# A second mixture of experts in which half of the tokens go to one expert per 128-row tile

## The chip, the cores and the metric

The kernel runs on one core of one Trainium2 chip. The metric is the device time of one launch in microseconds. The engines are called as the profile calls them: PE (matrix products and transposes), PEld (loading of PE's stationary operand), DVE and ACT (elementwise work), POOL (GpSimd), SP (the engine whose queue issues most DMAs). Everything is float32.

## The reference

The reference is a decoder of two layers on x of shape (32, 128, 128): 4096 tokens of 128 features. Each layer is an attention, a cross attention to a context of the same shape, and a mixture of experts, each behind a layer norm and added to x. Only the second layer's mixture matters here:

```
def _L1_ffn_ref(...):                      # x: layer norm of the tokens, (4096, 128)
    scores = x @ gate_w.T                  # (4096, 16); the 4 best experts of each token,
    ...                                    # a softmax over their 4 scores
    routed = sum over the 4 of  share * silu(x @ w1[e].T) * (x @ w3[e].T) @ w2[e].T
    shared = silu(x @ sw1.T) * (x @ sw3.T) @ sw2.T
    return routed + shared                 # 16 experts, all matrices 128 x 128
```

## The kernel before

A token block is 128 tokens, a group (`GB`) four blocks, 512 tokens; there are 8 groups, `x[0]` to `x[7]`, which stay in SBUF by token (128 partitions of tokens). The program runs in four stages on all groups: the first layer's two attentions (`first_layers`), its mixture (`mixture_layer`), the second layer's attentions (`second_layers`), and its mixture (`mixture_layer` again, the last stage).

`steps` writes a stage's order: each entry is (function, first step, every how many steps, how many times), and `between` entries fill in one vector operation at a time. In `second_layers`, from step 8 on, the order of PE, DVE, ACT and POOL is kept as it is written (`manual_schedule`); elsewhere the framework orders instructions by readiness and by their place in the program. Every engine, and SP's queue, works in order: an instruction that waits holds all behind it.

The second mixture (`mixture("l1f", ...)`) has these parts:

- `norm`, `scaled`, `turn`: the layer norm of a group (`bn_stats` on DVE, `power` on POOL, scaling half on DVE and half on POOL at L1106), and its transposes to features by tokens, `hx`.
- `routing` and `choose`: the products with the gate for two groups at a time (`NBR` = 8 blocks), and some 40 small DVE operations (`route_softmax`, `pick`) that find the four best of 16 experts and their shares. A generator is advanced a few operations per step.
- `send` and `fetch`: the shares are transposed, written to DRAM (`combined`) and read back, broadcast over 128 partitions (`share`, 1 MB per DMA).
- `experts(u)`: half a group's experts. For each of the 16 experts, and the shared one, on all 512 tokens of the group: two products of 512 columns into `pg` and `pu`, Silu on ACT (L1849), times `pu` on DVE (L1850), times the shares on DVE (L1852), and a third product that accumulates in `y`. After the last, `x` is added to `y` by four products with the identity, ACT copies and stores.

So every expert computes every token and the shares of the 12 not chosen are zero. The routing of groups 0 and 1 is done inside `second_layers`; that of the other groups inside the last stage, one pair of groups ahead. W1F, the weights of this mixture (3.3 MB), is loaded to SBUF once, before `second_layers`.

Of the kernel before, what the change touches and what calls it, by code (L numbers as in the profile page):

```python
# [17 lines left out]
GB = 4  # L18
# [57 lines left out]
def _layout(i):  # L76
# [44 lines left out]
        "later": {"b_o": rows(i["L1_xattn_b_o"], D), **_by_position("cos1", "sin1")},  # L121
# [820 lines left out]
def fast_decoder(ctx: ExitStack, tc: tile.TileContext, ins, spans, out: bass.AP):  # L942
# [6 lines left out]
    st = ctx.enter_context(tc.tile_pool(name="st", bufs=4))  # L949
    kinds = {}  # L950
# [8 lines left out]
    def mm(*args, **kw):  # L959
        last[0] = nc.tensor.matmul(*args, **kw)  # L960
# [29 lines left out]
    F = load("fast", nc.sync)  # L990
    ident = K["ident"]


    def load_wide(eng, *names):
        t = res.tile([128, sum(ins[n].shape[1] for n in names)], F32, name="wide")
        at, out = 0, []
        for n in names:
            part = t[:, at : at + ins[n].shape[1]]
            at += ins[n].shape[1]
            out.append((_Pieces(part, spans[n]), lambda part=part, n=n: eng.dma_start(out=part, in_=ins[n])))  # L1000
        return out

    (W0X, load_w0x), (W0F, load_w0f) = load_wide(nc.sync, "w0x", "w0f")
# [18 lines left out]
    ones_by_4 = res.tile([128, 4, 4 * HD], F32, name="ones_by_4")  # L1022
# [67 lines left out]
    def moments(src):  # L1090

        n = src.shape[1]
        parts = st.tile([128, n, 6], F32, name=f"parts{n}")
        mv = st.tile([128, n, 2], F32, name=f"mv{n}")
        for b in range(n):
            nc.vector.bn_stats(parts[:, b, :], src[:, b, :])
            nc.vector.bn_aggr(mv[:, b, :], parts[:, b, :])
            yield
        return mv
# [22 lines left out]
    def norm_factors(g):  # L1122
        mv = yield from moments(x[g])
        return mv, power(mv[:, :, 1], 1e-5, -0.5, "r")
# [488 lines left out]
    def first_layers(after):  # L1613
# [7 lines left out]
        rnorm, rscaled, rturn, routing, choose, send, _, _ = after  # L1621
# [42 lines left out]
                (lambda _: choose(0, 5), 30, 1, 11),  # L1664
                (xnormalize, 12, 2, NW, xweights),
# [7 lines left out]
    def pick(v, n, k, desc):  # L1673

        m = v.shape[1]
        eq = st.tile([128, m, n], F32, name=f"eq{n}", bufs=2)
        top = st.tile([128, m], F32, name=f"top{n}", bufs=2)
        for _ in range(k):
            nc.vector.tensor_reduce(top, v, AX.X, ALU.max)
            yield  # L1680
            nc.vector.tensor_tensor(eq, v, rep(top, n, 2), ALU.is_equal)
            yield
            nc.vector.tensor_tensor(eq, eq, rep(desc, m, 1), ALU.mult)
            yield
            nc.vector.tensor_reduce(top, eq, AX.X, ALU.max)
            yield
            nc.vector.tensor_tensor(eq, eq, rep(top, n, 2), ALU.is_equal)
            yield
            nc.vector.scalar_tensor_tensor(v, eq, -BIG, v, ALU.mult, ALU.add)
            yield  # L1690
# [77 lines left out]
    def mixture(tag, W, route, per, last):  # L1768
# [5 lines left out]
        xn, hs, combs, choices, weights, shares = {}, {}, {}, {}, {}, {}  # L1774

        def norm(wk, g):
            xn[g] = yield from norm_factors(g)

        def scaled(wk, g):
            xn[g] = yield from normed(wk, g, *xn[g])  # L1780

        def turn(wk, g):
            pool = edge if g in groups(0) else wk
            hs[g] = pool.tile([128, GT], F32, name="hx", bufs=2 if g in groups(0) else 5)
            by_feature(xn.pop(g), hs[g])

        def routing(wk, n):
# [4 lines left out]
            choices[n] = route(lg, edge)  # L1792
# [40 lines left out]
        def experts(wk, u):  # L1833

            g, half = divmod(u, 2)
            if half == 0:
                ys[g] = sums([128, GT], "y")
            y, h = ys[g], hs[g]
            for c in range(nch // 2) if half == 0 else range(nch // 2, nch + 1):
# [13 lines left out]
                mm(y, lhsT=wd, rhs=sg, start=(c == 0), stop=(c == nch and not last))  # L1853
            if half == 0:
                return
# [14 lines left out]
        return norm, scaled, turn, routing, choose, send, fetch, experts  # L1870

    def mixture_layer(tag, stages, more=()):
# [3 lines left out]
            lambda k, stage=stage: stage(wk, k) for stage in stages  # L1876
# [215 lines left out]
    def second_layers(stages, early, late, after):  # L2092
# [5 lines left out]
        rnorm, rscaled, rturn, routing, choose, send, _, _ = after  # L2098
        R = NBR // GB
# [3 lines left out]
        of_four = lambda stage, b, at: (lambda g: stage(g * GB + b), at + b, 4, NG)  # L2103

# [20 lines left out]
            (first(routing), 25, 1, 1),  # L2125
            (first(send), 43, 1, 1, choose),
# [7 lines left out]
                (lambda _: choose(0, 3), 26, 1, 13),  # L2134
            ],
            as_written=8,
        )

# [34 lines left out]
    edge = ctx.enter_context(tc.tile_pool(name="edge", bufs=1, reuse_waits="tile"))  # L2173
    flag = res.tile([1, 1], I32, name="flag")
    mixture0 = mixture("l0f", W0F, route_groups, 2, False)
    with scope():
        first_layers(mixture0)
    with tc.tile_pool(name="l1early", bufs=1, reuse_waits="tile") as early:
# [13 lines left out]
        ((W1F, load_w1f),) = load_wide(nc.sync, "w1f")  # L2192
        load_w1f()
        mixture1 = mixture("l1f", W1F, route_softmax, 1, True)
        with scope():
            second_layers(stages, early, late, mixture1)
    with scope():
        mixture_layer("l1f", mixture1, ((lambda wk, _: not_ok(wk), 9, 1, 1),))
# [35 lines left out]
```

## Time and profile before

| | us |
|---|---|
| median of 3 runs (lowest, highest) | 1500.13 (1499.58, 1506.42) |
| the profiled execution | 1502.94 |
| its span, first to last instruction | 1501.1 |
| mean granted PE clock | 0.963 of full |

The span by stage, from the trace, in us:

| stage | from | to | PE busy | DVE busy | POOL busy |
|---|---|---|---|---|---|
| second attention layers (from the load of W1F on) | 830 | 1112 | 240 | 181 | 108 |
| second mixture | 1112 | 1494 | 379 | 213 | 14 |
| end | 1494 | 1501 | 1.6 | 0 | 0 |

In the profile's groups a line reads: line, engine, operation, out<-in by the program's names, partitions x elements, count | busy us, mean ns of one | idle time of that engine just before them, and what ended it. Nearly all products have line L960, since one helper issues them. In the table of stretches the columns are the window, its length, each engine's busy time with its count, PE's granted clock, the busy share of the 16 DMA engines and GB/s. In the timeline the columns are start, duration, engine, line, operation. SPq is SP's queue, which issues DMAs; its rows give min/median/max duration in ns of the issue.

### The profile page before, as it was taken

To read this page: it belongs to the slowest core of one execution; us is meant where nothing else is said; L and a number is where in the kernel's file an instruction comes from. 1 tells how busy PE (TensorE), PEld (TensorE's weight loads), DVE (VectorE), ACT (ScalarE), POOL (GpSimd) and SP (SyncE) were. 2 spreads that over 40 slices of the span, in tenths; PEclk is the share of its full clock that TensorE was granted. 3 is DMA by queue.
4 is the path that set the end of the run, shared out by engine and by line. 5 is a ranking of instruction groups with operands and counts; after the bars stand their busy time and mean duration, and the time that the engine had idled before them with its cause. 6 is when DMAs were issued, how large, how long until landed. Compare 5 with 4: busy or idle time off the path is not lost.

```text
span 1501.1 us, 25599 instructions
## 1 busy us (share of the span) xinstructions
PE 1381.5 (92%) x10288; PEld 818.0 (54%) x10288; DVE 927.8 (62%) x2299; ACT 574.6 (38%) x842; POOL 355.3 (24%) x549
## 2 busy tenths in 40 slices
PE   3699999999999996999999898898689999999998
PEld 1367777777777775444444555565344444444443
DVE  5656767768686643757745466777556564564454
ACT  2354545454454332232322355555342222222221
POOL 5324343333422311320001254533330100000000
PEclk7799999999999997899999999999799999999999
DMA  6001211111121124351350100000022221322210
GB/s 242 1 1 30 57 31 30 30 30 31 30 49 39 30 49 105 71 114 41 74 114 13 78 2 2 2 2 2 2 115 98 96 96 70 121 84 93 107 75 9
DMA packets 36766, 85.01 MB, mean 57 GB/s; under 512 B 3232, under 2 KB 20128, under 8 KB 32160
## 3 DMA queue, kind: packets, MB, share of 16 engines
q1 hardware_dynamic: 35200, 80.68, 18.7%
q10 hardware_dynamic: 1440, 2.61, 0.5%
q8 instruction: 83, 1.36, 0.4%
q14 instruction: 43, 0.35, 0.1%
HBM read 80.40 MB, written 2.88 MB: 55 GB/s over the span
## 4 chain that ended last, share of the span: by engine, by line
PE 72%; DVE 14%; POOL 4%; ACT 4%; DMA 3%; issue 2%; SPq 1%; DVEq 0%; ACTq 0%; POOLq 0%
PE y L960 13%; PE pu L960 11%; PE pg L960 11%; PE po L960 7%; PE pqk L960 5%; PE scores L960 4%; PE sums L960 3%; PE xscores L960 3%; PE pval L960 2%; DMA factor<-factors 2%; PE proj L960 2%; PE xsums L960 1%; ACT e L1260 1%; DVE v L1525 1%; POOL xn L1106 1%
## 5 line engine op out<-in xcount | busy, mean ns | idle before, releaser
L1850 DVE TENSOR_TENSOR sg<-sg,pu 128x512 f32<-128x512 f32 x208 | 142.8, 687 | 223.1 <-PE pu L960 219.3
L1849 ACT ACTIVATE sg<-pg 128x512 f32<-128x512 f32 x208 | 124.2, 597 | 375.5 <-PE pg L960 356.6
L960 PE MATMUL y<-sg,wide 128*128 128x512 f32 x416 | 222.1, 621 | 4.2 <-DVE sg L1852 2.4
L960 PE MATMUL pg<-hx,wide 128*128 128x512 f32 x416 | 215.8, 601 | 0.0
L960 PE MATMUL pu<-hx,wide 128*128 128x512 f32 x416 | 214.8, 598 | 0.0
L1260 ACT ACTIVATE e<-scores 128x1024 f32<-128x1024 f32 x128 | 124.0, 1021 | 55.4 <-PE scores L960 55.4
L960 PEld LDWEIGHTS y<-sg,wide 128*128 128x128 f32 x416 | 64.7, 188 | 131.4 <-DVE sg L1852 107.4
L1852 DVE TENSOR_TENSOR sg<-sg,share 128x512 f32<-128x512 f32 x192 | 132.5, 690 | 4.8
L960 PEld LDWEIGHTS pu<-hx,wide 128*128 128x128 f32 x416 | 79.1, 192 | 95.2 <-issue 93.6
L960 PEld LDWEIGHTS pg<-hx,wide 128*128 128x128 f32 x416 | 78.1, 192 | 89.7 <-issue 87.9
L1106 POOL TENSOR_SCALAR xn<-x,mv,r 128x128 f32<-128x128 f32 x96 | 80.6, 847 | 158.0 <-PE pxn L1115 82.8
L1275 DVE STREAM_TRANSPOSE by_token<-sums 128x512 f32<-128x512 f32 x64 | 45.6, 713 | 81.3 <-PE sums L960 81.0
L1511 ACT ACTIVATE e<-xscores 128x1024 f32<-128x1024 f32 x64 | 62.0, 1021 | 79.9 <-PE xscores L960 79.9
L960 PE MATMUL scores<-qb,k 32*128 32x512 f32 x512 | 75.5, 660 | 11.4 <-ACT qb L1446 4.0
L960 PE MATMUL sums<-e,v 128*32 128x128 f32 x2048 | 73.8, 285 | 12.7 <-POOL v L1056 10.6
L960 PEld LDWEIGHTS sums<-e,v 128*32 128x32 f32 x2048 | 54.7, 113 | 40.5 <-issue 15.0
L1525 DVE COPY v<-pval 128x512 f32<-128x512 f32 x64 | 43.5, 680 | 50.6 <-PE pval L960 50.6
L960 PE MATMUL po<-e,v 128*64 128x128 f32 x1024 | 65.0, 279 | 7.6 <-DVE v L1525 7.6
L1559 ACT COPY av<-po 128x512 f32<-128x512 f32 x64 | 37.5, 586 | 88.3 <-PE po L960 88.3
L960 PE MATMUL po<-av,wide 128*128 128x256 f32 x256 | 64.1, 406 | 7.7 <-DVE av L1579 7.7
L1490 DVE COPY qk<-pqk 128x512 f32<-128x512 f32 x64 | 43.4, 685 | 39.8 <-PE pqk L960 39.6
L1115 PE MATMUL pxn<-in_few,xn 128*128 128x128 f32 x192 | 37.0, 302 | 33.3 <-DVE xn L1106 21.9
(218 smaller groups left out, 2237.2 us busy)
## 6 DMA issues: line engine op xcount, KB each, us to landing
share<-combined SPq DMA_DIRECT2D x32, 1024.0 KB, 4.7
factor<-factors SPq DMA_DIRECT2D x64, 256.0 KB, 4.9
share<-combined SPq DMA_DIRECT2D x32, 512.0 KB, 12.0
wide<-in_w1f_dram SPq DMA_DIRECT2D x1, 3272.0 KB, 10.4
wide<-in_w0x_dram SPq DMA_DIRECT2D x1, 2112.0 KB, 10.4
x<-in_xt_dram SPq DMA_DIRECT2D x8, 256.0 KB, 5.5
ctx<-in_ctx_dram SPq DMA_DIRECT2D x8, 256.0 KB, 8.1
out_dram<-y ACTq DMA_DIRECT2D x8, 256.0 KB, 2.0
```

Source lines behind the costliest of these rows:

```text
L960: last[0] = nc.tensor.matmul(*args, **kw)
L1106: eng.tensor_scalar(n[:, b, :], x[g][:, b, :], mv[:, b, 0:1], r[:, b : b + 1], ALU.subtract, ALU.mult)
L1115: nc.tensor.transpose(pt[:, b, :], n[:, b, :], ident)
L1260: nc.scalar.activation(e[-1], ps[:, bass.ts(n, 2)].rearrange("p c i s -> p (c i) s"), AF.Exp, scale=scale)
L1275: nc.vector.transpose(tt.rearrange("p i t r -> p (i t r)"), po.rearrange("p i s -> p (i s)"))
L1490: nc.vector.tensor_copy(t, ps)
L1511: nc.scalar.activation(e[-1], ps[:, n].rearrange("p r c s -> p (r c) s"), AF.Exp, scale=scale)
L1525: nc.vector.tensor_copy(v[:, bass.ts(n, XC), :], pv)
L1559: nc.scalar.copy(avs[w][n][:, :, bass.ts(b, S)], po)
L1849: nc.scalar.activation(sg, pg, AF.Silu)
L1850: nc.vector.tensor_tensor(sg, sg, pu, ALU.mult)
L1852: nc.vector.tensor_tensor(sg, sg, shares[g][c // NS][:, c % NS], ALU.mult)
```

## The change

Groups 0 to 3 (`BY_ROWS` = 4 groups, 16 blocks) no longer go through all experts. Each of their tokens is written four times, by indirect DMA, to rows of a DRAM buffer ordered by expert, each expert's rows starting at a multiple of 128. That makes at most 4 x 16 + 16 = 80 tiles of 128 rows (`NT`), each of one expert, in 20 `QUADS` of four; the number is fixed whatever the routing. A quad is loaded, its four experts' matrices are loaded from DRAM by an expert number that SP reads into a register, and the results go to a second DRAM buffer. From there each token's four rows are gathered by indirect DMA, weighted with the shares and added to `x`. The shared expert and the store of these groups follow. Groups 4 to 7 go through all experts as before.

```diff
+    def filled(q):                                     # 20 of these, in first_layers, one a step from step 14
+        nc.sync.dma_start(out=four_tiles(rows_in, q), in_=rep(ident, 4, 1))
...
+        def route(lg, n):                              # for blocks 0 and 1 (groups 0 to 3)
...
+            for k in range(4):
+                yield from pick(v, E, 1, K["desc16"], ones[:, k, at])
+                t = st.tile([128, NBR, E], F32, name=f"eq{E}", bufs=2)
+                nc.vector.tensor_tensor(t, ones[:, k, at], s, ALU.mult)
+                nc.vector.tensor_reduce(raw[:, :, k], t, AX.X, ALU.add)
...
+        def places(_):                                 # row of each token and choice, expert of each tile
+            pos = sm([128, NB + 1, E], "places")
+            mm(pos, lhsT=L["below"], rhs=mask, start=True, stop=False)
+            for b in range(NB):
+                mm(pos[:, b + 1 :], lhsT=one.to_broadcast([128, 128]), rhs=rep(mask[:, b], NB - b, 1), ...)
...                                                     # some 20 DVE operations on 128x256
+        def way_out(u):                                # u: block, 0 to 15, after the steps of second_layers
...
+            nc.vector.tensor_scalar(t, x[g][:, b, :], mv[:, b, 0:1], r[:, b : b + 1], ALU.subtract, ALU.mult)
+            for k in range(4):
+                sent = nc.gpsimd.indirect_dma_start(
+                    out=rows_in,
+                    out_offset=bass.IndirectOffsetOnAxis(ap=place[:, k, u : u + 1], axis=0),
+                    in_=t, in_offset=None)
...
+        def weights(wk, q):                            # all on SP's queue, kept in this order
+            xq = wk.tile([128, 4, D], F32, name="rows", bufs=3)
...
+                sent = nc.sync.dma_start(out=xq, in_=four_tiles(rows_in, q))
+            for j in range(4):
+                with tc.issue_after(sent.ins):
+                    e = nc.sync.value_load(owner[0:1, 4 * q + j : 4 * q + j + 1], min_val=0, max_val=E - 1)
+                    w = wk.tile([128, 3, S], F32, name="row_weights", bufs=12)
+                    sent = nc.sync.dma_start(out=w, in_=every[:, :, bass.ds(e, 1), :].rearrange("p k e f -> p (k e) f"))
...
+        def experts(wk, q):
+            for j in range(4):
+                nc.tensor.transpose(pt[:, j], xq[:, j], ident)
+            nc.vector.tensor_copy(h, pt)
+            for i, p in enumerate((pg, pu)):
+                for j, w in enumerate(ws):
+                    mm(p[:, j], lhsT=w[:, i], rhs=h[:, j], start=True, stop=True)
+            nc.scalar.activation(sg, pg, AF.Silu)
+            nc.vector.tensor_tensor(sg, sg, pu, ALU.mult)
+            for j, w in enumerate(ws):
+                mm(py[:, j], lhsT=sg[:, j], rhs=w[:, 2], start=True, stop=True)
+            nc.scalar.copy(y, py)
+            nc.scalar.dma_start(out=four_tiles(rows_out, q), in_=y)
...
+        def way_back(wk, u):
+            t = wk.tile([128, 4, D], F32, name="back", bufs=4)
+            for k in range(4):
+                nc.gpsimd.indirect_dma_start(out=t[:, k], out_offset=None, in_=rows_out,
+                    in_offset=bass.IndirectOffsetOnAxis(ap=place[:, k, u : u + 1], axis=0))
+            for k in range(4):
+                nc.vector.scalar_tensor_tensor(xb, t[:, k], share[:, u, k : k + 1], xb, ALU.mult, ALU.add)
...
+    def last_layer(tag, stages, rows_stages):          # in place of mixture_layer for the second mixture
+        steps(                                         # G0 = 4, R = 2, n = 3
+            (lambda i: fetch(G0 + i), 0, 1, 1),
+            (lambda i: turned(G0 + R + i), 0, 1, R),   # norm, scaled, turn of groups 6, 7
+            (lambda _: fetch(G0 + 1), 0, 1, 1),
+            (lambda _: routing(n), 1, 1, 1),
+            (lambda _: stages[4](n), 1, 1, 1),
+            (again, 1, 1, G0),                         # scaled and turn of groups 0 to 3 once more
+            (lambda _: send(n), 3, 1, 1),
+            (lambda i: fetch(G0 + R + i), 3, 1, R),
+            (weights, 4, 1, QUADS),
+            (row_experts, 4, 1, QUADS),
+            (way_back, 4 + QUADS, 1, NB),
+            (lambda u: experts(2 * G0 + u), (0, 1, 2, 3, 4 + QUADS, 8 + QUADS, 12 + QUADS, 16 + QUADS), 1, 2 * (NG - G0)),
+            (shared, 8 + QUADS, 4, G0),
+            (rest, 8 + QUADS, 4, G0),
+            (lambda _: not_ok(wk), 6, 1, 1),
+        )
...
     def second_layers(stages, early, late, after, rows_stages):
-        R = NBR // GB
+        R = BY_ROWS + NBR // GB                        # norm, scaled, turn of 6 groups here, not 2
...
-            (first(routing), 25, 1, 1),
-            (first(send), 43, 1, 1, choose),
+            (first(routing), 25, 8, 3),
+            (places, 38, 1, 1, choose_1),
+            (lambda _: send(early, 2), 44, 1, 1, choose_2),
...
-                (lambda _: choose(0, 3), 26, 1, 13),
+                (lambda _: choose(0, 8), 26, 1, 6),
+                (choose_1, 34, 1, 4),
+                (choose_2, 42, 1, 3),
             ],
             as_written=8,
         )
+        for u in range(NB):
+            way_out(u)
```

Not shown: three small constant tables are added to a load, some buffers move between pools, and the layer norm's factors of groups 0 to 3 are kept for `way_out` and `again`.

## The prediction

> **What bounds the kernel now.** I read the page first, then busy time by stage, then the last stage's groups, then single rows for the prices of what the change adds.
>
> ```profile
> span 1501.1 us, 25599 instructions
> PE 1381.5 (92%) x10288; PEld 818.0 (54%) x10288; DVE 927.8 (62%) x2299; ACT 574.6 (38%) x842; POOL 355.3 (24%) x549
> ...
> PE 72%; DVE 14%; POOL 4%; ACT 4%; DMA 3%; issue 2%; SPq 1%; DVEq 0%; ACTq 0%; POOLq 0%
> ```
>
> PE carries 72% of the chain that ended last; POOL is idle for three quarters of the span.
>
> ```profile
> core 0: us, PE busy (x) PEld busy (x) DVE busy (x) ACT busy (x) POOL busy (x), PEclk, DMA share, GB/s
> 830.00:1112.00 282.00, 240.34 (x3094) 157.78 (x3094) 180.76 (x522) 146.14 (x198) 108.18 (x171) 0.95 0.02 5
> 1112.00:1494.00 382.00, 378.89 (x970) 161.34 (x971) 212.70 (x397) 101.67 (x165) 14.02 (x19) 1.00 0.25 94
> 1494.00:1501.00 7.00, 1.62 (x10) 1.05 (x8) 0.00 (x0) 0.58 (x1) 0.00 (x0) 0.79 0.14 48
> ```
>
> The second mixture is the stage from 1112 us on, 389 us to the end. PE works in 379 of its first 382 us at full clock, POOL in 14. The second attention layers (830 to 1112) leave PE 42 us and DVE 101 us of idle time.
>
> ```profile
> L960 PE MATMUL y<-sg,wide 128*128 128x512 f32 x272 | 145.7, 621 | 1.1 <-DVE sg L1850 0.9 <-DVE sg L1852 0.2
> ...
> L1850 DVE TENSOR_TENSOR sg<-sg,pu 128x512 f32<-128x512 f32 x136 | 93.5, 687 | 156.7 <-PE pu L960 155.6 <-ACT sg L1849 0.7
> ```
>
> 272 records are 136 products of 512 columns, two records each: 8 groups of tokens times 17 experts (16 and the shared one). DVE waits for PE, not PE for DVE, so PE sets the end of this stage. Starts of successive products give the pace:
>
> ```profile
> 1480.32 1.02 PE L960 MATMUL y<-sg,wide 128*128 128x512 f32 x2
> ...
> 1481.17 1.02 PE L960 MATMUL pu<-hx,wide 128*128 128x512 f32 x2
> ...
> 1482.03 1.02 PE L960 MATMUL pg<-hx,wide 128*128 128x512 f32 x2
> ```
>
> 0.86 us a product, 2.58 us for the three of one unit (one expert, 512 tokens); 136 units are 351 of the 389 us.
>
> **The change: PE.** Groups 0 to 3 lose 16 of 17 units: 64 x 2.58 = 165 us less. In their place come 20 quads of four 128-row tiles: 12 products of 128 columns and 4 transposes each.
>
> ```profile
> 1067.38 1.06 PE L960 MATMUL proj<-in_w1x,aT 128*128 128x128 f32 x8
> ...
> 806.60 1.04 PE L1974 MATMUL prot<-in_few,rot 128*128 128x128 f32 x8
> ```
>
> Four products of 128 columns with weights of their own take 1.06 us, so 12 take 3.2 us; transposes are one record each, eight in 1.04 us, so four take 0.5 us: 3.7 us a quad, 74 us for 20. DVE (one copy of 0.68, one product of 0.69 us) and ACT (0.60 and 0.59 us) have less per quad and lie beside it. If PE stayed the bound, the stage would lose 91 us. But three new things stand in a row around the quads.
>
> **SP and the DMA engines, per quad.** SP loads 256 KB of rows, and four times reads an expert's number into a register and issues a 192 KB load of its three matrices.
>
> ```profile
> L1829 SPq DMA_DIRECT2D share<-combined x64: 319/515/1307, 588.8 to 1444.7; - x64
> ...
> L2207 SPq COMPARE_BRANCH  x1: 45/45/45, 1445.7 to 1445.7; - x1
> ```
>
> An issue takes about 0.5 us (0.61 for the factors' DMAs). The last issue of SP ends at 1445.04 and the branch on a register filled from SBUF comes at 1445.7, so a register read costs at most 0.66 us. One tile: 1.2 us, a quad 4 x 1.2 + 0.5 = 5.3 us; address arithmetic has no row, I take 6.0. The bytes are 26.2 MB (15.7 weights, 5.2 in, 5.2 out) in 51,200 packets of 512 B, a size the trace lacks:
>
> ```profile
> 14.00:18.00 4.00, 4.00 (x8) 1.96 (x8) 1.64 (x6) 0.80 (x3) 3.51 (x8) 0.67 1.05 400
> ...
> q1 hardware_dynamic: 1113, 1.06, 52.5%
> ```
>
> The first row is loads in 2 KB packets at 400 GB/s; at that rate a quad takes 3.3 us. The second is 1113 packets of about 1 KB in 9 us (the factors at 503 to 512): 0.525 x 9 x 16 / 1113 = 68 ns each. Were a 512 B packet no cheaper, 2560 of them over 16 engines take 10.9 us a quad. Ends: 3.7 us (PE's pace) and 10.9 us; I take SP's 6.0, because the two DMA rows differ in how many partitions they fill as well as in size: 120 us for 20 quads.
>
> The Trainium skill (DMA: Bandwidth & Descriptors, Specifications) calls 512 B the least transfer that runs at line rate and gives 358 GB/s as the HBM limit of a core; an estimate by it is 73 us for the 26.2 MB, and SP would stay the bound. No run here shows 512 B packets yet.
>
> **POOL, 64 transfers out and 64 back, 128 rows of 512 B each.** The trace has no DMA issued by POOL. Per transfer the low end is the 0.34 us of the ACT queue's issue of 128 rows (out_dram); the high end is one at a time until landed, 2.0 us by the same DMA's median, 2.9 by its longest.
>
> ```profile
> L1079 POOL TENSOR_TENSOR r<-r,half 128x4 f32<-128x4 f32 x19 | 19.6, 1034 | 1.3
> ...
> L1308 POOL TENSOR_TENSOR x<-x,bias1x 128x512 f32<-128x512 f32 x8 | 10.2, 1273 | 4.4 <-DVE xn L1106 4.0
> ```
>
> POOL pays 1.03 us even for 4 elements a partition of its heavy operation, 1.27 for 512 of a light one. I take 1.27, the row with work on all 128 partitions: 81 us each way. The way out is covered by the full experts of groups 4 and 5 (34 units, 88 us, and some 10 us of routing, transposes and first share load: 98 us). Were that cover gone, 81 us would be on the path. The first row load on SP waits for all 64 scatters, and all weights are queued behind it.
>
> The way back can only start when the last quad has landed (7 us for its products and its 2.0 us store). Beside it stand the full experts of groups 6 and 7, the four shared units and eight groups' adds of x: 38 x 2.58 + 8.4 + 7 at the end = 113 us. Where PE fills its holes between the quads with that work ahead of time, the gathers alone remain, 81 + 8 (landing, sums, transposes, copy, store) = 89 us. I take 100.
>
> The same page of the skill (Anatomy of one DMA; Rules for kernel authors) speaks against the change: it gives about 2.0 us fixed per transfer from GpSimd plus bytes over 436 GB/s, and counts what is under 64 KB as mostly overhead; these are 64 KB each. Were each transfer to hold POOL for the 2.15 us that this gives, the time would be 1543 us by the sum below. No run here shows it.
>
> **What moves ahead of 1112.** Routing of blocks 1 and 2 goes into the attention layers: 94 DVE operations of about 0.29 us, 27 us; the places add some 20 operations, 8 us; scaling four groups 3 us: 38 us against 101 us of idle. On PE 34 records for the places (5 us), 32 for logits (4) and 16 transposes (2): 11 us. PE's order is fixed there and PE is the bound, so 11 us show; of DVE's 38 I let a fifth show, since the norms of that tail already held PE for 6.5 us at 1081: 19 us. Ends: 0 (all in the idle time) and 49. Turning groups 0 to 3 again costs PE 2 us, in the 98. The 20 fills of rows_in (first layers) cost nothing: SP waits there for DVE (332 us in all) and DMA is 14% busy; without that cover each would hold the factors by some 1.6 us.
>
> **Sum.** 19 + 98 + 120 + 7 + 100 = 344 us where 389 were: 45 us less. The profiled execution took 1502.94 us (span 1501.1 and 1.8 around it), 2.8 above the median 1500.1; off the median, 1455.
>
> **Rivals.** *Quads at PE's pace* (registers read ahead, packets near 400 GB/s, cheap transfers): 19 + 98 + 74 + 7 + 113 = 311, 78 less, 1422; 1403 if the moved routing hides too. For it: DMA is 25% busy here. Against: SP's issue rows. *POOL becomes the bound, slower*: with c us per indirect transfer the stage is 19 + (64c + 2) + 120 + 7 + (64c + 8); it equals 389 at c = 1.82, and decides from 1.5 on, where 64c + 2 passes 98. At 2.0 us 1523, at 2.4 (between the two landings) 1574. For it: POOL's slow rows and each transfer's 128 separate rows; against: POOL need not wait for landing. *Packets of 512 B as dear as 1 KB*: with q us a quad 19 + 98 + 20q + 7 + 89 equals 389 at q = 8.8; at 8.5 1494, no change; at 10.9 1542. *The change does not do what it says*: the tile count is fixed at 80 whatever the routing, so the work on PE drops in any case; I give this none.
>
> **How the numbers follow.** Forecast 0.44, PE's pace 0.20, POOL 0.24, dear packets 0.12. About 0.5% (7.5 us) can be told from no change. Faster: 0.42 of the forecast and 0.20: 0.62. Same: 0.02 of the forecast, 0.01 of POOL, 0.04 of packets: 0.07. Slower: 0.31. The range 1405 to 1560 leaves out POOL above 2.3 us (0.13) and the best end of PE's pace (0.05). The forecast's own range is 1430 to 1480 (quads of 5 to 7 us).
>
> **What would show it.** Right: PE about half busy in the quads with "row_weights" as releaser, the SP queue issuing every 1.2 to 1.5 us, POOL issuing scatters through the first 80 us of the stage and gathers through the last 80. Wrong: indirect issues on POOL over 1.8 us apart, PE over 90% busy in the quads, DMA share near 1 there, or the attention layers ending after 1160 us.

## The result and the profile after

The changed kernel takes 1595.2 us (median of 4 runs, 1593.0 to 1598.4) against 1502.8 for the kernel before: ratio 1.0616, 95% interval 1.0579 to 1.0653. It is slower by 92 us where 45 us less was predicted. Its profiled execution spans 1596.6 us. From its page:

```profile
span 1596.6 us, 26812 instructions
PE 1328.9 (83%) x10499; PEld 833.7 (52%) x10499; DVE 901.7 (56%) x2333; ACT 555.3 (35%) x814; POOL 488.7 (31%) x685
...
PE 62%; DVE 17%; another core or an unknown queue 6%; POOL 5%; issue 4%; DMA 3%; ACT 3%; SPq 1%; DVEq 0%; ACTq 0%; POOLq 0%
...
L2076 POOL DMA_INDIRECT back<-rows_out,place x64 | 62.9, 983 | 154.9 <-DMA rows_out<-yrows 130.5
...
L2020 POOL DMA_INDIRECT rows_in<-y,place x64 | 62.4, 976 | 19.7 <-issue 18.3
```

PE has 53 us less to do, as intended, and still ends 95 us later: its share of the chain of waits fell from 72 to 62%, and an entry is new that the kernel before does not have, 6% "another core or an unknown queue". There is one core, so this is an engine that waited for a signal whose source the profile cannot name. The last two rows are the indirect DMAs: 0.98 us of POOL each.

The stage by stretches (columns as before: length, busy time of each engine, PE's granted clock, DMA share, GB/s):

```profile
1112.00:1217.00 105.00, 38.05 (x273) 19.02 (x273) 20.74 (x68) 14.98 (x19) 66.48 (x77) 0.60 0.12 38
1217.00:1316.50 99.50, 97.58 (x267) 43.48 (x267) 57.95 (x123) 29.43 (x48) 11.44 (x14) 0.99 0.44 155
1316.50:1424.00 107.50, 75.84 (x576) 65.90 (x575) 28.61 (x43) 24.85 (x42) 0.00 (x0) 1.00 0.83 222
1424.00:1594.00 170.00, 122.24 (x277) 50.37 (x275) 65.38 (x134) 26.20 (x44) 62.90 (x64) 0.87 0.18 61
```

First the scatters with the end of the attention layers, then the full experts of groups 4 and 5, the quads, and the way back. Against the prediction's sum, in us:

| part | predicted | measured |
|---|---|---|
| from 1112 to the first quad | 19 + 98 = 117 | 204.5 |
| 20 quads | 120 | 107.5 |
| drain and way back, to the end | 7 + 100 = 107 | 172.6 |
| sum (389.1 before) | 344 | 484.6 |

The first stretch is the worst: PE works 38 of 105 us, POOL alone is busy. The cover (the experts) runs after the scatters instead of beside them. Two kinds of wait fill the stretch. The timeline has both (start, duration, what ran, and in brackets the idle time before it and what ended it):

```profile
1147.49 1.93 PE L969 MATMUL sums<-e,v 128*32 128x128 f32 x32 [18.49 <-POOL v L1067]
...
1164.00 0.72 DVE L1286 STREAM_TRANSPOSE by_token<-sums 128x512 f32<-128x512 f32 x1 [33.39 <-remote]
...
1199.73 0.29 DVE L1752 COPY s<-logits 128x128 f32<-128x128 f32 x1 [34.05 <-remote]
...
1199.88 1.94 ACT L1271 ACTIVATE e<-scores 128x1024 f32<-128x1024 f32 x2 [65.63 <-remote]
```

In the first line PE waits 18 us for `v`, a copy of 0.3 us on POOL. POOL's own rows say why: the copy stands behind a run of scatters.

```profile
1142.52 0.96 POOL L2020 DMA_INDIRECT rows_in<-y,place  x1 [0.30 <-issue]
...
1147.14 0.76 POOL L1067 COPY v<-vs 128x128 f32<-128x128 f32 x3
```

In the other three, DVE and ACT wait 33 to 66 us for something "remote". The chain of waits (start, length) has five pieces of this sort, 90 us in all; the four longest:

```profile
1130.61 33.37 another core or an unknown queue
...
1165.68 34.02 another core or an unknown queue
...
1491.25 12.71 another core or an unknown queue
1506.66 7.14 another core or an unknown queue
```

The first two, and the fifth of 2.7 us, lie in the scatters (1107 to 1194), the last two in the gathers (1428 to 1515).

### The profile page after: what moved, and what is told of

Its sections match the earlier page's. It is cut to its first block, busy times and chain, and to the rows that moved or that the text cites. A ratio compares the mean times of both kernels' runs of the same rounds, so it can differ in the third digit from the quotient of the medians.

```text
span 1596.6 us, 26812 instructions
## 1 busy us (share of the span) xinstructions
PE 1328.9 (83%) x10499; PEld 833.7 (52%) x10499; DVE 901.7 (56%) x2333; ACT 555.3 (35%) x814; POOL 488.7 (31%) x685
## 4 chain that ended last, share of the span: by engine, by line
PE 62%; DVE 17%; another core or an unknown queue 6%; POOL 5%; issue 4%; DMA 3%; ACT 3%; SPq 1%; DVEq 0%; ACTq 0%; POOLq 0%
PE y L969 8%; PE pg L969 8%; PE pu L969 7%; PE po L969 7%; PE pqk L969 5%; PE scores L969 4%; PE sums L969 3%; PE xscores L969 3%; PE pval L969 2%; DMA factor<-factors 2%; PE proj L969 2%; POOL back L2076 1%; PE xsums L969 1%; PE pyrows L969 1%
## 5 line engine op out<-in xcount | busy, mean ns | idle before, releaser
L969 PE MATMUL y<-sg,wide 128*128 128x512 f32 x288 | 159.6, 645 | 47.7 <-DVE sg L1876 34.0
L1874 DVE TENSOR_TENSOR sg<-sg,pu 128x512 f32<-128x512 f32 x144 | 98.7, 686 | 168.7 <-PE pu L969 136.1
L1873 ACT ACTIVATE sg<-pg 128x512 f32<-128x512 f32 x144 | 86.0, 597 | 305.9 <-PE pg L969 242.2
L969 PE MATMUL pg<-hx,wide 128*128 128x512 f32 x288 | 155.2, 622 | 0.0
L969 PE MATMUL pu<-hx,wide 128*128 128x512 f32 x288 | 152.6, 612 | 0.0
L2076 POOL DMA_INDIRECT back<-rows_out,place x64 | 62.9, 983 | 154.9 <-DMA rows_out<-yrows 130.5
L969 PEld LDWEIGHTS pu<-hx,wide 128*128 128x128 f32 x288 | 56.7, 199 | 69.5 <-issue 67.5
L1876 DVE TENSOR_TENSOR sg<-sg,share 128x512 f32<-128x512 f32 x128 | 88.0, 689 | 2.5
L969 PEld LDWEIGHTS pg<-hx,wide 128*128 128x128 f32 x288 | 55.8, 200 | 63.3 <-issue 61.5
L2020 POOL DMA_INDIRECT rows_in<-y,place x64 | 62.4, 976 | 19.7 <-issue 18.3
```

What stands on the lines that cost most here:

```text
L1873: nc.scalar.activation(sg, pg, AF.Silu)
L1874: nc.vector.tensor_tensor(sg, sg, pu, ALU.mult)
L1876: nc.vector.tensor_tensor(sg, sg, shares[g][c // NS][:, c % NS], ALU.mult)
L2020: sent = nc.gpsimd.indirect_dma_start(out=rows_in, out_offset=bass.IndirectOffsetOnAxis(ap=place[:, k, u : u + 1], axis=0), in_=t, in_offs ...
L2076: nc.gpsimd.indirect_dma_start(out=t[:, k], out_offset=None, in_=rows_out, in_offset=bass.IndirectOffsetOnAxis(ap=place[:, k, u : u + 1], ...
```

## The experiments

The theories, as the expectations name them: **A**, an indirect DMA costs POOL's time and whoever stands behind it in an in-order queue, nothing else; **B**, the stream slows all other work beside it; **C**, a dense stream makes signals between the other engines late, by 8 to 50 us at a time; **D**, each such DMA delays its neighbours, at any density.

An overview first. "Late" is the sum of the chain's pieces put down to an unknown queue, in the profiled execution. In e7 and e11 the chain breaks off close to the end, and in e15 and e17 it does not reach back to the scatters; the figures there are from the waits of DVE and ACT. The six runs with idle streams begun early differ from e1 in when the streams start, in their pace, and e14 in the form of its scatters. The runs differ in one more thing: e1 to e4 were measured together, in one sitting on one chip, e5 to e8 in a second on the same chip, e9 to e12, e13 to e16, and e17 with e18 in three more, each on another chip. Every ratio is to the kernel before in the same sitting.

| run | ratio to before (95%) | late, us: scatters, gathers |
|---|---|---|
| after; e5, the same again | 1.062; 1.058 (1.051 to 1.065) | 70, 20; 73, 19 |
| e1 before + idle indirect streams | 0.999 (0.995 to 1.003) | 0, 0 |
| e2 the same, plain DMAs | 1.001 (0.998 to 1.004) | 0, 0 |
| e3 after, scatters later | 1.042 (1.039 to 1.046) | 0, 0 |
| e4 after without the sums | 1.008 (1.005 to 1.011) | 0, 0 |
| e6 after, POOL work for scatters | 1.039 (1.032 to 1.046) | no scatters, 23 |
| e7 e3 with `again` later | 1.053 (1.046 to 1.061) | see below |
| e8 e7 + sums later | 1.057 (1.049 to 1.064) | 45, 31 |
| e9 e8 paced 1.69 us | 1.044 (1.040 to 1.048) | 0, 0 |
| e10 e8 paced 1.38 us | 1.039 (1.033 to 1.046) | 23, 0 |
| e11 e7, plain scatters | 1.014 (1.008 to 1.020) | 0, 21 |
| e13 routing first, 14 buffers | 1.042 (1.037 to 1.047) | 50, 32 |
| e12 before + idle streams, early | 1.092 (1.088 to 1.097) | 141 in both |
| e16 the same, 12 us later | 1.090 (1.084 to 1.095) | 104 in both |
| e14 early, plain scatters | 1.038 (1.033 to 1.043) | 0, 64 |
| e15 early, scatters paced 1.69 us | 1.056 (1.050 to 1.061) | 0, 57 |
| e17 early, both paced 1.69 us | 1.019 (1.014 to 1.023) | 0, 0 |
| e18 early, both in runs of eight | 1.014 (1.009 to 1.020) | 0, 0 |

### Does the stream slow its neighbours? (e1, e2)

To the kernel before, 64 scatters and 64 gathers of 128 rows were added in the last mixture's second half; nothing reads what they move. In e2 the same with plain 64 KB DMAs.

```diff
+            sent = nc.gpsimd.indirect_dma_start(out=rows_in,
+                out_offset=bass.IndirectOffsetOnAxis(ap=bench["place"][:, u : u + 1], axis=0),
+                in_=bench["src"], in_offset=None)
...
+            nc.gpsimd.dma_start(out=rows_in[bass.ts(u, S), :], in_=bench["src"])      # e2
...
+        (lambda wk, _: burst_out(wk), 8, 1, 1), (lambda wk, _: burst_back(wk), 10, 1, 1)
```

> The kernel before, with 64 indirect scatters and then 64 indirect gathers of 128 rows by 512 bytes put on POOL's queue in the second half of the last mixture. No product, no activation and no other operation reads what they write, so its results are those of the kernel before. Theory A (queue order: an indirect DMA costs POOL's time and the wait of whoever stands behind it in a queue): within 8 us of the kernel before, since nothing stands behind them; PE stays at about 20 us busy in each 20 us. Theory B (stream: while POOL issues these DMAs one after another, the other engines hardly go on): PE falls to about 4 to 10 us busy in 20 from some 20 DMAs into each burst, as in 1160 to 1200 of the changed kernel, and the kernel is 80 to 130 us slower than before.

> The same as the run with 64 indirect scatters and gathers in the last mixture, with plain 64 KB DMAs from POOL's queue in their place (fixed rows, no index). Theory A: as the kernel before, within 8 us. Theory B, if any DMA issued by POOL does it: as slow as the indirect ones, 80 to 130 us over the kernel before. Theory B, if it is the index form: within 8 us of the kernel before.

Neither costs anything in this sitting. Stretches of e1, POOL busy with the stream in both:

```profile
1300.00:1320.00 20.00, 20.00 (x64) 9.69 (x63) 16.86 (x47) 7.04 (x10) 15.43 (x16) 1.00 0.47 165
1400.00:1420.00 20.00, 20.00 (x47) 8.07 (x46) 10.36 (x16) 4.78 (x8) 15.43 (x16) 1.00 0.39 122
```

PE is busy 20.00 of 20 us at full clock. Sixteen DMAs in 20 us are 1.27 us each, the prediction's price; plain ones took 0.54 us of POOL. B falls: experts can run beside a stream at full speed. This said nothing yet of why the real kernel has late signals.

### POOL's order (e3, e4, e6)

e3 takes the scatters out of the attention layers' program and puts them into step 1 of the last stage:

```diff
-        for u in range(NB):
-            way_out(u)                     # end of second_layers
+            (out_all, 1, 1, 1),            # steps of last_layer
```

> The changed kernel with its 64 scatters emitted in the last mixture's step 1 instead of at the end of the attention layers: on POOL's queue they stand behind all work of the attention layers and the normalized rows of groups 6 and 7, and beside the full experts of groups 4 and 5. Theory A: attention ends near 1131, scatters 1130 to 1215 beside 98 us of experts, quads begin near 1235 instead of 1316: about 1515 us. Theory B: the experts of groups 4 and 5 lose some 55 to 70 us to the scatters, quads begin near 1290: about 1565 to 1585 us.

The attention layers now end at about 1141 instead of 1218, PE works 20.00 of 20 us beside the first scatters, and the chain has no late signal. But the next POOL work is behind the scatters instead: scaling half of groups 0 to 3 once more (`again`). The waits of e3's PE between 1140 and 1300 (total, times, longest):

```profile
PE pxn L1126 <- POOL xn L1117: 42.9, 3, 41.5
```

So the quads start at 1283.7, 33 us earlier than after. The whole takes 1565 us, which is B's figure and not A's 1515, but for these reasons and the sums below, not for B's. e6 leaves the scatters' places and replaces each by an addition on POOL, which took 1.05 us on average:

```diff
-                sent = nc.gpsimd.indirect_dma_start(out=rows_in, ...)
+                nc.gpsimd.tensor_tensor(t, t, t, ALU.add)
```

> The changed kernel with each scatter replaced by a POOL addition on 128x512 of some 1.27 us (left out: the tokens' rows are not sent, quads run on the fill). POOL's queue has the same work of the attention layers in the same places between them, and no scatter is on any DMA queue. Theory A (queue order on POOL): PE waits for POOL's copies of v as long as before, quads begin about 100 us after the last of these additions as they did after the last scatter of the run without the additions to x, and the kernel takes 1560 to 1590 us. Theory B (the stream of scatters slows the others): attention ends near 1131, quads begin near 1235, the kernel takes about 1510 us.

Its quads start at 1274.0, against 1316.5 after and 1229 by the prediction's sum. The longest wait of its PE between 1050 and 1280 (total, times, longest):

```profile
PE sums L969 <- POOL v L1067: 30.4, 3, 17.5
```

So 45 of the 87 us lost are there with no DMA on the way out. POOL's order is some 30 of them. The other 15 are the work moved ahead of 1112: e3 and e11 (below), with no scatter in the attention layers, start the experts at 1141 and 1150, not at 1131 as the sum has it. The remaining 42 come with the real DMAs: late signals, 70 us of the chain there, and perhaps some of POOL's time, since the scatters stand 1.27 us apart. e4 drops the weighted sums of the gathered rows, to free DVE:

```diff
-            for k in range(4):
-                nc.vector.scalar_tensor_tensor(xb, t[:, k], share[:, u, k : k + 1], xb, ALU.mult, ALU.add)
```

> The changed kernel without the four additions of gathered rows to x for each block (64 DVE operations; left out: the experts' part of groups 0 to 3). The gathers stay and nobody waits for them. Theory A: what holds the end is DVE standing at these additions until rows land, ahead of the experts' own operations; without them the stretch after the quads falls from 172 us to about 113, and the kernel to about 1537 us. Theory B: the gathers themselves slow the others; the stretch stays at 155 us or more, the kernel at 1575 us or more.

Its way back takes 113 us, PE's figure in the prediction, where after takes 173. In e4's gathers PE is at full pace:

```profile
1440.00:1460.00 20.00, 20.00 (x47) 8.04 (x46) 10.35 (x15) 4.78 (x8) 15.43 (x16) 1.00 0.22 64
```

In the same stretch, with the sums, after had:

```profile
1440.00:1460.00 20.00, 9.69 (x14) 3.75 (x15) 8.53 (x22) 1.20 (x2) 15.43 (x16) 0.77 0.22 68
```

DVE is far from full there (8.53), but its order is fixed: a sum that waits for its gathered rows holds the experts' products behind it. e3 shows this without any late signal; its DVE from 1391 to 1500:

```profile
DVE x L2084 <- DMA back<-rows_out,place: 48.1, 32, 5.6
DVE sg L1874 <- PE pu L969: 14.3, 8, 3.9
```

48 us of waiting for rows, and a way back of 163 us, 50 over e4. e4's scatters, in their old places, had no late signals either, only waits for POOL's `v` (36 us in three); its quads start at 1280.8, 52 us over the sum. That agrees with e6: 30 to 36 us of POOL's order in 45 to 52.

### Again, and mending the order (e5, e7, e8, e13)

> The changed kernel itself once more, beside the other runs of this chip: 1590 to 1600 us. Open in it is the stretch 1130 to 1199, in which ACT and DVE stood for 65 and 34 us and PE issued one 128x128 product in 2 us though their inputs were there, and which the run without the additions does not show though its scatters are the same. If it belongs to this kernel, it is there again with some 40 us in which no engine but POOL goes on for a reason that the profile names; if not, quads begin some 20 us sooner after the last scatter (124 us in the first run of this kernel, 102 in the run without the additions).

The same kernel again: the same start of the quads (1316.8) and nearly the same sum of late signals, but in other places (6, 9, 35 and 23 us in the scatters). So the wait is not bound to one instruction.

e7 is e3 with `again` moved to step 8, behind the scatters' end; e8 adds back buffers and emits the sums later:

```diff
-            (again, 1, 1, G0),
+            (out_all, 1, 1, 1),
+            (again, 8, 2, G0),
...                                       # e8
-            t = wk.tile([128, 4, D], F32, name="back", bufs=4)
+            t = wk.tile([128, 4, D], F32, name="back", bufs=8)
+            (adds, 11 + QUADS, 4, G0),
```

> The changed kernel with the scatters in the last mixture's step 1 as in the earlier run of that kind, and with the normalized rows of groups 0 to 3 for the shared expert (POOL xn, PE pxn) made from step 8 on, in the quads, so that PE does not stand behind the scatters on POOL's queue. Theory A: the 41 us that PE waited for xn there go, quads begin right after the experts of groups 4 and 5, and the kernel takes 1565 - 41 = 1524 us. Theory B: PE loses the time to the scatters anyway, 1550 us or more.

> The run with late scatters and late xn, and in addition eight buffers for gathered rows instead of four, and the additions to x emitted a group at a time 7 steps after the gathers, beside the last experts, so that DVE does not stand at them ahead of the experts' own operations. Theory A: the stretch after the quads falls from 163 to 172 us to 115 to 125, the kernel to 1524 - 45 = about 1480 us, under the kernel before. Theory B (gathers slow the others): no change from the run with late scatters and late xn, about 1520 to 1550.

Both fell short of A's figures, by 59 and 103 us. The orders are mended and the wait for POOL is gone, but now the full experts beside the scatters meet late signals. The waits of e7 (total, times, longest):

```profile
DVE sg L1874 <- remote: 67.1, 6, 18.1
ACT sg L1873 <- remote: 63.7, 5, 16.3
```

Eight hops from PE to ACT or DVE come 2 to 18 us late while the scatters run, four 8 to 16 us late in the gathers. A alone is not enough. e13 tries the best order I knew: routing of groups 6 and 7 first, then the scatters beside nothing but experts, 14 back buffers, sums last.

```diff
+            (routed, 0, 1, 1),                  # turn and routing of groups 6, 7
+            (out_all, 1, 1, 1),
+            (lambda _: send(n), 6, 1, 1),
+            (again, 9, 2, G0),
+            (adds, 17 + QUADS, 1, G0),
```

> The changed kernel put in another order: routing of groups 6 and 7 first in the last mixture, then the scatters beside the experts of groups 4 and 5 with no other signals between the engines; their shares sent, and xn for the shared expert, in the quads; 14 buffers for gathered rows, and the additions to x behind expert 7 (blocks 0 to 3) or 12 of group 7. Theory A, and if only experts run beside the streams as in the two undisturbed runs: scatters 1165 to 1247, quads 1255 to 1362, gathers 1366 to 1448, additions and shared experts 25 to 30 us behind the last experts: 1485 to 1495 us. Theory C without that condition: 1540 us or more, with PE at 5 to 10 us in 20 in one of the streams.

It fell too, at 1567 us for 1485 to 1495: 50 us of late signals in the scatters, 32 in the gathers. Plain experts beside the stream do not protect.

### What of the stream does it (e11, e9, e10)

e11 is e7 with plain DMAs to fixed rows in place of the scatters:

```diff
-                sent = nc.gpsimd.indirect_dma_start(out=rows_in, out_offset=..., in_=t, in_offset=None)
+                sent = nc.gpsimd.dma_start(out=rows_in[bass.ts(4 * u + k, S), :], in_=t)
```

> The run with late scatters and late xn, with each scatter replaced by a plain 64 KB DMA from POOL's queue to fixed rows (left out: the order by expert; quads run on these rows). If the index form makes the delays, the experts of groups 4 and 5 run at full pace beside the stores, quads begin near 1245 and the kernel takes 1583 - 60 = about 1520 us. If any stream of DMAs from POOL does it, PE stands again for some 60 us or, since these are 0.55 us each and end after 35 us, for some 25: 1550 us or more.

Two stretches of e11, in the scatters:

```profile
1160.00:1180.00 20.00, 20.00 (x61) 9.44 (x60) 13.11 (x29) 4.26 (x8) 14.17 (x27) 1.00 0.88 278
1180.00:1200.00 20.00, 20.00 (x46) 8.17 (x46) 17.47 (x46) 7.17 (x12) 16.08 (x31) 1.00 0.84 274
```

The quads start at 1246.8, 60 us before e7's. The same bytes at twice the rate, with the DMA engines busy to 0.84 and more, disturb nobody; the indirect form does at a DMA share of 0.12 (the first stretch after). In e11 itself the gathers, still indirect, bring two late waits of DVE, 11.6 and 9.4 us. So it is not bandwidth, and it is the index form, or the scattered rows that come with it: the plain DMAs wrote 128 rows in a block, and no run separates the two. e9 and e10 put a memset on POOL behind each indirect DMA of e8:

```diff
+        def pause(pool, sent):
+            t = pool.tile([128, 4 * S], F32, name="pause", bufs=2)     # e10: [128, 128]
+            with tc.issue_after(sent.ins):
+                last.append(nc.gpsimd.memset(t, 0.0).ins)
```

> The run with late scatters, late xn and late additions, with a POOL memset of 128x512 after each indirect DMA, so that they come half as densely (some 2.2 us apart instead of 1.27). Theory C (a dense stream delays the signals between the other engines, by 8 to 35 us at a time once it has lasted some 15 DMAs): with half the density no engine stands without a reason that the profile names, PE is at 20 us in 20 until the experts of groups 4 and 5 end, quads begin when the stream ends, 1148 + 141 = about 1290, and the gathers take 141 us: about 1390 + 141 + 25 = 1550 us. Theory D (it is not the density: each such DMA costs the others some time): PE stays at 5 to 10 us in 20 through both streams, 1600 us or more.

> The same with a POOL memset of 128x128 after each indirect DMA, some 1.6 to 1.7 us apart. Theory C: the delays go or shrink; scatters 105 us beside 98 us of experts, quads from 1148 + 108 = 1256, gathers 105 us, 1256 + 107 + 105 + 20 = about 1490 us. Theory D: as the run without the pauses (1583 us) or slower, by the longer streams.

At 1.69 us a DMA no late signal is left, at 1.38 there are 23 us for e8's 45 in the scatters and none for its 31 in the gathers. Both miss theory C's figures (1570 us for 1550, 1562 for 1490). The gain in time is small in e9: the streams now last 108 us each, its routing order gives DVE a plain wait of 48 us on a DMA, and the sums wait for rows.

### The disputed cost by itself (e12, e14 to e18)

e12 is e1 begun one routing earlier, in a later sitting; nothing depends on the streams.

```diff
-            if last and g == NG - 1:           # where the index table is made
+            if last and g == 5:
...
-        (lambda wk, _: burst_out(wk), 8, 1, 1),
+        (lambda wk, _: burst_out(wk), 4, 1, 1),
```

> The kernel before with the 64 idle scatters four steps earlier in the last mixture, beside the routing of groups 4 to 7 (small DVE operations and signals between PE, DVE, ACT and POOL), gathers as in the run of that kind before. Theory A: within 8 us of before, as in that run. Theory C, if what it takes is many signals between the engines beside the stream: engines stand without a named reason in the scatters' 81 us and the kernel is 20 to 60 us slower than before.

135 us more, for DMAs that nobody waits for, where C was put at 20 to 60. Stretches of e12:

```profile
1180.00:1200.00 20.00, 20.00 (x50) 8.31 (x48) 10.54 (x19) 5.25 (x9) 15.52 (x15) 1.00 0.57 207
1200.00:1220.00 20.00, 9.66 (x40) 5.18 (x38) 2.02 (x3) 1.18 (x2) 15.22 (x16) 0.87 0.35 119
1220.00:1240.00 20.00, 0.00 (x0) 0.00 (x0) 0.00 (x0) 0.00 (x0) 15.12 (x17) 0.50 0.16 52
```

PE, DVE and ACT stand still for 20 us and more while POOL goes on at its even pace. What ended it, in e12's timeline:

```profile
1204.27 1.86 PE L961 MATMUL logits<-wide,hx 128*128 128x16 f32 x16
...
1251.31 0.29 DVE L1739 COPY s<-logits 128x128 f32<-128x128 f32 x1 [48.95 <-remote]
```

PE's logits are done at 1206, and DVE, idle, starts on them 45 us later. Late loading of the program's instructions is not the reason here: four late waits end between 1250 and 1277, and no packet of the `instruction` queues moves from 1207 to 1277. In e1, with the same step inside its stream, DVE waited 0.93 us. This is theory C by itself. e16 begins the scatters 12 us later, e14 has plain scatters and indirect gathers, e15 paces the scatters alone:

```diff
+                for _ in range(12):                                  # e16: before the first scatter
+                    nc.gpsimd.tensor_scalar(t[:, 0:D], bench["src"], 1.0, None, ALU.mult)
...
+            nc.gpsimd.dma_start(out=rows_in[bass.ts(u, S), :], in_=bench["src"])   # e14
...
+                paused.append(nc.gpsimd.memset(t, 0.0).ins)          # e15: t is [128, 512]
```

> The run with idle scatters beside the routing of groups 6 and 7 (1638 us), its scatters begun some 10 us later behind 13 small POOL operations. If the delays come wherever the stream meets this much routing: 1630 to 1645 us again. If it is a matter of where the two meet (the same stream one routing later did nothing at all): anything between the kernel before and that, most likely under 1600 us.

> The run of the kernel before with idle scatters beside the routing of groups 6 and 7 (1638 us), with plain DMAs for the scatters; the idle gathers, some six steps of experts later in the program, stay indirect. If the index form is what delays the signals: no delay beside the plain ones; whether the gathers alone do it is open: within 10 us of the kernel before if not, 40 to 70 us over it if they do.

> The same with indirect scatters, each followed by a POOL memset of 128x512, so that they come 1.7 us apart instead of 1.27; gathers as before. Theory C (density): no delay in the scatters, and 40 to 70 us in the gathers at most: 1500 to 1570 us instead of 1638. Theory D (each such DMA delays the others): as slow as 1638 us or slower.

e16 costs the same (1637.0 and 1637.7 us) with its late signals in other places, so it is no coincidence with one instruction. e14 and e15 keep PE at 20.00 beside plain and beside paced scatters, but for a plain wait of 18 us for POOL's `xn` at the end of e15's, and their unpaced gathers cost 64 and 57 us of late signals: gathers do it as well. e15's 1587 us is above C's 1500 to 1570 and below D's 1638. The last two pace both streams, evenly and in runs of eight with 3.3 us after each:

```diff
+        if k % 8 == 7:                          # e17: after each DMA, once; e18: after eight, six times
+            for _ in range(6):
+                paused.append(nc.gpsimd.memset(t, 0.0).ins)
```

> The kernel before with 64 idle indirect scatters and 64 idle indirect gathers begun early (nothing reads what they move), now with a 541 ns memset on GpSimd behind every one of the 128: a pace of some 1.69 us instead of 1.27. With neither stream paced this cost +135 us; with the scatters alone paced 1579.9 us of span, of which the gathers' late signals were 16.0 + 35.0 + 6.0 = 57 and a plain wait for GpSimd's xn behind the scatters 18. Theory C (a dense stream makes signals late, a thinner one does not): no late signals at all, so 1580 - 57 = 1523, some 1.5% over before, the 18 us of the plain wait being all that is left; the gathers take 108 us. Theory D (each indirect DMA delays its neighbours, whatever the pace): the stalls come back spread out, 1560 to 1640.

> The same idle streams, early, but the pause gathered: eight indirect DMAs at full pace (8 x 1.27 = 10 us), then six 541 ns memsets (3.3 us), and so on: 2.0 pauses of 1.69 us less than half as long on average as the even pace, 13.4 us per eight, 1.68 us per DMA on average, as in the evenly paced one. If the average pace decides: as the evenly paced one, some 1523. If the pace from one DMA to the next decides (several close together are enough): late signals again, between 1560 and 1637. If a run of more than eight is needed to begin (the stalls began 12 to 18 DMAs into a stream): 1523 as well, so only a slow result tells these apart from the density alone.

Both do as theory C said (spans of 1523.5 and 1517.9 for 1523): no late signals, D falls. What is left over before is mostly a plain wait for POOL's `xn` behind the scatters, 18 and 14 us. A stretch of e17 and one of e18, each in the gathers:

```profile
1340.00:1360.00 20.00, 19.95 (x47) 8.23 (x47) 13.26 (x28) 7.05 (x10) 18.12 (x24) 1.00 0.40 141
```

```profile
1360.00:1380.00 20.00, 19.92 (x52) 8.36 (x50) 8.99 (x14) 4.79 (x9) 16.61 (x22) 1.00 0.35 120
```

The same 128 indirect DMAs cost 135 us at 1.27 us apart (e12), 26 us at 1.69 (e17) and 19 us at 1.66 on average with eight close together (e18). So eight in a row were not enough; that the average rate over some longer run counts would fit. But e17 and e18 had a sitting of their own, with no dense stream to compare. What pacing does is shown within one sitting by the scatters of e15 (paced, no late signal) and e16 (dense, 31 us of late signals in the chain), and by e9 against e12.

**What stays open.** Why a dense stream makes signals late, and why not always: e1, e3 and e4 ran both streams at 1.27 us undisturbed. Start time, neighbours and kind of work beside it did not sort these from e7, e12 and e13. The sitting does: e1, e3 and e4 are of the first one, and none of their six dense streams has a late signal; in `after` and the later sittings all 18 dense streams have some, on the same chip too (e5 to e8). So the harmless runs may say something of the sitting and nothing of the kernel; e1 was not run again in a later one, which would have told. That signals between engines share a path with the streams' completions or descriptors would fit; no run shows it. No complete version beat the kernel before; the best were e10, e3 and e13 at 1.04 times its time, e3 in the sitting without late signals. e4 and e11 leave part of the work out.

## Why the prediction was wrong

**Three prices were right, and a fourth by luck.** An indirect DMA of 128 rows: 1.27 us predicted from POOL's row of 1273 ns, 1.27 measured, so the rival "POOL becomes the bound", which needed 1.82, did not happen, nor did POOL stand for the 2.15 us at a time that the prediction worked out against the change. The Trainium skill (Perfetto Trace Analysis, DMA Instruction — SWDGE) says that such a row ends when the descriptors are written, not when the data has landed. The trace agrees: in e3 the first gather's row ends at 1396.74, and the sum that waits for its rows starts at 1398.21. PE's work on the way back: 113 predicted, behind 7 of drain, and 113 with the drain measured in e4. The full experts of groups 4 and 5: 98 predicted, 97.9 measured (1218.6 to 1316.5).

A quad: 6.0 predicted, 107.5 / 20 = 5.4 measured, within the forecast's 5 to 7, and 512 B packets reached 222 GB/s. But the 6.0 was SP's pace of issue, with PE "about half busy" and "row_weights" as releaser. In the quads after PE works 75.8 of 107.5 us (71%), 3.8 us a quad where 3.7 were predicted, and nearly all the rest is two waits (total, times, longest):

```profile
PE pyrows L969 <- DVE sgrows L2064: 16.4, 19, 1.0
PE pg L969 <- DVE hrows L2057: 14.9, 19, 0.8
```

PE never waits for rows or weights there. DVE's copy and product, 0.7 us each, stand between PE's products, where the prediction had them "lie beside it". That 5.4 came out near 6.0 is luck.

**Step that failed first: "the way out is covered by the full experts of groups 4 and 5".** I costed the 81 us on POOL and named their cover, but not where they stand in POOL's order. They were put into it as soon as the places were known, among the tail of the attention layers, ahead of POOL's copies of `v` and scalings that PE's fixed order needs first. So the cover came after the scatters. The prediction even priced this ("were that cover gone, 81 us would be on the path") and then gave it no chance of its own. Measured in e6: 45 us on the sum of 117, of which PE waits 30 for POOL's `v`. The other 15 are a term that was too small, the 19 us for what moves ahead of 1112: 29 and 38 us in e3 and e11.

**Second: "I take 100" for the way back.** It took PE's 113 and POOL's 89 as the two ends of a range, two things side by side. The 64 sums join them: on DVE in program order, each waits for its rows ahead of the experts' products. Measured in e3: 50 us over e4. So DVE, 62% busy before and never PE's bound, became the place where the gathers' pace reaches PE.

**Third, not in the prediction at all: late signals beside the streams.** 42 us before the quads (after, and e5, against e6) and 20 us in the gathers by the chain; no view of the kernel before has a row of this sort. Only a run could show it: e12. Why signals come late stays open.

The sum of the misses: 45 + 42 before the quads, -12.5 for the quads, and 66 on the way back (6 of PE's 113 against 107, 50 for the sums' order, some 10 of the 20 us of late signals, since the two waits overlap) are 141 us, the distance from 344 to 485.

Of the signs that the prediction named for being wrong, "the attention layers ending after 1160 us" came true (1218), and of those for being right, "POOL issuing scatters through the first 80 us" was seen as well; it was no sign of success.

## What to carry to other kernels

A cover counts only if it can run at that time: for each operation added to an in-order engine, ask what is queued behind it there (POOL's 0.3 us copies, DVE's products), not just how busy the engine is. Before building on a long stream of indirect DMAs, add it idle to the old kernel at several times and on more than one occasion (e1 alone would have cleared it), and look for waits without a name; if there are any, pace the stream, since 1.69 us apart it made no signal late here. A price that proves right to the percent says nothing of the sum if the place in the order is wrong.

## What the runs showed of the hardware

- An indirect DMA of 128 rows of 512 B mostly holds POOL for 0.94 to 0.98 us, 1.25 to 1.27 us apart, scatter or gather (after, e1); a plain one of the same 64 KB 0.54 us (e2).
- Beside 64 indirect DMAs at 1.27 us, engines' signals to each other came up to 45 us late (DVE's `s` in e12), with the DMA engines 16% busy; beside plain ones with them 84 to 88% busy none did (e11). In one sitting (e1, e3, e4) none did beside indirect ones either.
- PE's granted clock is 0.50 in a 20 us stretch in which it stands still (e12, e14), and 0.93 to 1.00 in the first one after that in which it is busy for all 20 us (0.93 in e14, 1.00 in e12).
